# Local attention stack: ScalarE's copies ahead of the norm, the variance later in its step, three feed-forward tiles in the larger PSUM pool

## The chip, the core and the metric

The kernel runs on one core of one Trainium2 chip. The core has a matrix engine (TensorE, PE in the profile, its weight loads PEld), VectorE (DVE), ScalarE (ACT), GpSimd (POOL) and SyncE (SP, which here only issues transfers). Each engine takes its own instructions in the order of the program and waits for others on semaphores. [...]

The metric is the device time of one execution in microseconds. Before the change three runs gave 1410.27, 1412.57 and 1418.48; the median is 1412.57.

## The reference

`reference(x, ...)` is a decoder block over x of shape (2, 512, 128). It has three parts, each with a residual and a layer norm: a state-space layer with a mixture of experts, a cross attention, and a stack of local attention. The change touches only the third part, which takes more than half of the time. Cut to what matters:

```python
for i in range(6):                                   # DEPTH
    x = attn_layer(shift_tokens(x), Wqkv[i], ...) + x   # 16 heads of 64, windows of 32
    x = ffn_layer(shift_tokens(x), ln_g[i], ...) + x

def attn_layer(x, Wqkv, qs, ksc, Wo):
    q, k, v = split(x @ Wqkv)                        # 3 x 1024
    q, k = rotary(l2norm(q) * qs), rotary(l2norm(k) * ksc)
    # softmax(8 q k') v, each window of 32 looking at itself and the one before
    return local_attention(q, k, v) @ Wo

def ffn_layer(x, g, bln, W1, b1, W2, b2):
    mu = x.mean(-1); var = ((x - mu) ** 2).mean(-1)
    xn = (x - mu) / sqrt(var + 1e-5) * g + bln
    a, gate = split(xn @ W1 + b1)                    # 2 x 341
    return a * gelu(gate) @ W2 + b2
```

## The kernel before

All is float32. The activations lie transposed: 128 features on the partitions, tokens along the free axis. A tile is 128 tokens of one of two sequences, so a layer has eight tiles and six layers have 48. The stack is a software pipeline written out by hand, under a manual schedule: step s issues work for tile s (called A: projection, rotation, norms, values), for tile s-1 (B_: transposes of q and k, scores, softmax) and for tile s-2 (C: transposes of p, attention with v, transposes of o, output projection). The order of the calls in the step is the order on every engine.

After the last of the four tiles of a sequence a feed-forward begins. It takes two steps: F1, the step after, with `mean` and `var`, and F2, the next one, with `spread`, `hidden` and `out`. F2's `out` writes z, the input of the next layer's tiles. So the steps come in fours: F1, F2, and two without a feed-forward; I call such a group a block, and there are twelve, the last in the drain of the pipeline.

PSUM is split in two pools. `psa` has three buffers of two banks (128 x 1024 floats, tag "a"), which in a step go in turn to the q projection, the k projection, two attention outputs, the scores and the values. `psb` has two buffers of one bank (tag "b"), which go in turn to everything else: pairs of transposes, the FFN's mean, variance, spread, hidden pieces and outputs. A new tile waits until the readers of the tile that held its buffer before have finished.

What the change and the prediction touch, by line:

- `project` (L921, two projections of q and k on TensorE), `square` (L926, ScalarE), `rotate` (L933 and L937 on VectorE, the sum L942 on GpSimd), `sums` (L946, VectorE). rotate(0) is q's, rotate(1) k's.
- `norm`: ScalarE L964, L888, L889; GpSimd L965 and L890 to L893; then two products of 128x1024 on GpSimd (L968), whose results the next step's transposes of q and k (L1101) read.
- `values`: TensorE L954, ScalarE's copy L956, then two transfers issued by SP.
- `flip_p`, `flip_q`, `flip_k`: transposes L1101 and ScalarE's copies L1102. `flip_o`: transposes L1072, ScalarE's copies L1074 and L1076 to oT. `out` of a tile: L1091, every second tile, and VectorE L1094.
- `scores` L995 and L1006, `softmax` L1017 and L1019 on VectorE, `expo` L1023 on ScalarE, `attend` L1042, `weigh` L1056 and L1057 on VectorE.
- FFN: `mean` (`centre`: L1107, L1108, L1110), `var` (`rstd`: matmuls L1117, ScalarE L1119, L888, L889, GpSimd L890 to L893, giving ln_rs), `spread` (matmuls L1129 into ln_sd, VectorE L1147, GpSimd L1148), `table` (a table load on ScalarE, L1151), `hidden` (three chunks of 128, 128 and 85; each has a gate piece fg_ps L1158, a value piece fa_ps L1160, Gelu L1162 on ScalarE and the product L1163 on VectorE), `out` (L1172, L1175).

The end of the step as it was, with what the diff moves:

```python
A.norm()          # ScalarE, GpSimd
C.flip_o()        # TensorE, ScalarE
B_.expo()         # ScalarE
F1.var()          # TensorE, ScalarE, GpSimd
F2.out()
A.values()        # TensorE, ScalarE, SP
F1.table()
C.out()
```

Of the kernel before, what the change touches and what calls it, by code (L numbers as in the profile page):

```python
# [11 lines left out]
F32 = mybir.dt.float32  # L12
# [9 lines left out]
B, S, D = 2, 512, 128  # L22
NT = B * S
P = 128
# [8 lines left out]
INNER = H * DH  # L33
# [33 lines left out]
def decoder_kernel(ctx: ExitStack, tc: tile.TileContext, t: dict, out: bass.AP):  # L67
# [75 lines left out]
    def col(i, n=P):  # L143
        return cols[0:n, i : i + 1]
# [12 lines left out]
    def rstd(ss, name, scale=1.0 / D):  # L157

        v = fp.tile([P, NTB], F32, tag="v4", name=f"{name}_v", bufs=2)
        r = fp.tile([P, NTB], F32, tag="r4", name=f"{name}_r", bufs=2)  # L160
        na = fp.tile([P, NTB], F32, tag="n4", name=f"{name}_n", bufs=2)
        nc.gpsimd.tensor_scalar(v, ss, scale, EPS, ALU.mult, ALU.add)
        nc.gpsimd.tensor_tensor(r, v, mhalf.to_broadcast([P, NTB]), ALU.pow)
        nc.gpsimd.tensor_mul(na, v, r)
        nc.gpsimd.tensor_mul(na, na, r)
        nc.gpsimd.tensor_scalar(na, na, -0.5, 1.5, ALU.mult, ALU.add)
        nc.gpsimd.tensor_mul(r, r, na)
        return r
# [650 lines left out]
    def load_layer(i):  # L819
        wqkv = lw.tile([P, 3 * INNER], F32, tag="wqkv", name=f"wqkv_{i}")  # L820
        for j in range(3):
            sl = slice(j * INNER, (j + 1) * INNER)
            nc.sync.dma_start(out=wqkv[:, sl], in_=t["L0_ffn_Wqkv"][i][:, sl])
        wo = lw.tile([P, INNER // P, D], F32, tag="wo", name=f"wo_{i}")
        nc.sync.dma_start(out=wo, in_=t["L0_ffn_Wo"][i].rearrange("(c p) d -> p c d", p=P))
        w1 = lw.tile([P, 2 * DFF], F32, tag="w1", name=f"w1_{i}")
        nc.sync.dma_start(out=w1, in_=t["L0_ffn_W1"][i])
        w2 = lw.tile([P, 3, D], F32, tag="w2", name=f"w2_{i}")
        nc.sync.dma_start(
            out=w2[:, 0:2, :], in_=t["L0_ffn_W2"][i][0:256].rearrange("(c p) d -> p c d", p=P)  # L830
        )
        nc.sync.dma_start(out=w2[0 : DFF - 256, 2, :], in_=t["L0_ffn_W2"][i][256:DFF])

        qs = lw.tile([P, 4, DH], F32, tag="qs", name=f"qs_{i}", bufs=1)
        nc.sync.dma_start(out=qs, in_=t["qks"][i : i + 1].to_broadcast([P, 4, DH]))
        tab = lw.tile([P, 4, 4, DH], F32, tag="tab", name=f"tab_{i}")
        return wqkv, wo, w1, w2, tab, qs

    def scale_tables(layer):
        tab, qs = layer[4:]  # L840
        nc.gpsimd.tensor_mul(tab, rot, qs.unsqueeze(2).to_broadcast([P, 4, 4, DH]))
# [13 lines left out]
    psa = ctx.enter_context(tc.tile_pool(name="lpsa", bufs=3, space=PSUM))  # L855
    psb = ctx.enter_context(tc.tile_pool(name="lpsb", bufs=2, space=PSUM))
# [38 lines left out]
    def exp_ln_table():  # L895
        tc.keep_in_program_order(nc.scalar.preload_act_table_set("natural_log_exp_and_others"))
# [206 lines left out]

    def centre(dst, src):

        pm = psb.tile([P, S], F32, tag="b", name="ln_mean")
        mm(pm, ones_inv, src, start=True, stop=True)  # L1107
        nc.vector.tensor_sub(dst, src, pm)  # L1108
        sq = ftmp.tile([P, S], F32, tag="fsq", name="ln_sq")
        nc.scalar.activation(sq, dst, AF.Square)  # L1110
        return sq
# [12 lines left out]

    def spread(rs):

        sd = psb.tile([P, S], F32, tag="b", name="ln_sd")
        for n in range(NTB):
            mm(sd[:, n * P : (n + 1) * P], rs[:, n : n + 1].to_broadcast([P, P]), ident, start=True, stop=True)  # L1129
        return sd  # L1130

    class Ffn:
# [5 lines left out]
        def mean(self):  # L1138
            self.xc = ftmp.tile([P, S], F32, tag="xc", name="ln_xc")
            self.sq = centre(self.xc, za[:, self.b, 1 : 1 + S])  # L1140
# [4 lines left out]
        def spread(self):  # L1145
            xc, i = self.xc, self.i
            nc.vector.scalar_tensor_tensor(xc, xc, col(C_LNG + i), spread(self.rs), ALU.mult, ALU.mult)  # L1147
            nc.gpsimd.tensor_scalar_add(xc, xc, col(C_LNB + i))  # L1148
# [4 lines left out]
        def hidden(self):  # L1153
            i, xc, w1 = self.i, self.xc, self.w1
            hid = self.hid = ftmp.tile([P, 3, S], F32, tag="hid", name="fhid")
            for c, (f0, fs) in enumerate(FCH):
                pg = psb.tile([P, S], F32, tag="b", name="fg_ps")
                mm(pg[0:fs], w1[:, DFF + f0 : DFF + f0 + fs], xc, start=True, stop=True)  # L1158
                pa = psb.tile([P, S], F32, tag="b", name="fa_ps")
                mm(pa[0:fs], w1[:, f0 : f0 + fs], xc, start=True, stop=True)  # L1160
                ge = ftmp.tile([P, S], F32, tag="ge", name="ge", bufs=2)
                nc.scalar.activation(ge[0:fs], pg[0:fs], AF.Gelu, bias=col(C_B1 + 6 * i + 3 + c, fs))  # L1162
                nc.vector.scalar_tensor_tensor(  # L1163
                    hid[0:fs, c, :], pa[0:fs], col(C_B1 + 6 * i + c, fs), ge[0:fs], ALU.add, ALU.mult
                )
            exp_ln_table()
# [20 lines left out]
    with tc.manual_schedule(engines={ET.PE, ET.Activation, ET.DVE, ET.Pool}):  # L1187
        for s in range(len(tiles) + 5):
            A = B_ = C = None
            if s < len(tiles):  # L1190
                i, b, ti = tiles[s]
                if (b, ti) == (0, 0) and i + 1 < DEPTH:
                    layers[i + 1] = load_layer(i + 1)
                if (b, ti) == (1, 0) and i + 1 < DEPTH:
                    scale_tables(layers[i + 1])
                A = live[s] = Tile(s, i, b, ti, layers[i], live.get(s - 1))
            B_, C = live.get(s - 1), live.pop(s - 2, None)

            F1, F2 = ffns.get(s - 1), ffns.get(s - 2)
            if B_:  # L1200
                B_.keys_before()
            if A:
                A.begin()
                A.project(0)
                A.square(0)
            if F1:
                F1.mean()
            if F2:
                F2.spread()
            if A:  # L1210
                A.rotate(0)
            if C:
                C.flip_p()
            if A:
                A.project(1)
                A.square(1)
                A.rotate(1)
            if B_:
                B_.flip_q()
            if C:  # L1220
                C.attend()
                C.weigh()
            if B_:
                B_.flip_k()
            if A:
                A.sums(0)
                A.sums(1)
            if F2:
                F2.hidden()
            if B_:  # L1230
                B_.scores()
                B_.softmax()
            if A:
                A.norm()
            if C:
                C.flip_o()
            if B_:
                B_.expo()
            if F1:
                F1.var()  # L1240
            if F2:
                F2.out()
            if A:
                A.values()
            if F1:
                F1.table()
            if C:
                C.out()
                if C.ti == NTB - 1:
                    ffns[s] = Ffn(C.i, C.b, C.layer)  # L1250

    for b in range(B):
        y = ftmp.tile([P, S], F32, tag="xc", name="fin")
        for h0, at in ((0, 1), (64, 2)):
            nc.vector.tensor_add(
                y[h0 : h0 + 64], xT[h0 : h0 + 64, bs(b)], z[h0 : h0 + 64, b, at : at + S]
            )
        sd = spread(rstd(centre(y, y)))
        nc.vector.tensor_mul(y, y, sd)
        pt = psb.tile([P, 4, D], F32, tag="b", name="fin_t")  # L1260
        for n in range(4):
            tr(pt[:, n, :], y[:, n * P : (n + 1) * P], ident)
        yo = ftmp.tile([P, 4, D], F32, tag="ge", name="yo", bufs=2)
        nc.vector.tensor_copy(yo, pt)
        nc.sync.dma_start(out=out[b].rearrange("(n p) d -> p n d", p=P), in_=yo)
# [127 lines left out]
```

## Time and profile before

| | |
|---|---|
| median of three runs | 1412.57 us |
| profiled execution, its own time | 1412.37 us |
| its span, first to last instruction | 1410.6 us |
| mean granted TensorE clock | 0.910 |
| TensorE busy between 549 and 1330 us | 710.30 of 781.00 us |
| VectorE, ScalarE, GpSimd busy there | 496.18, 412.52, 430.80 us |
| first projection of tile 0, of tile 47 | 402.62 us, 1306.45 us |

The span is divided among engines by busy time. A busy share says how much of an engine's time is filled, not what ends last; that is read from the chain of waits (each piece is what the next one waited for) and from the timeline of one engine, where a bracket gives the idle time before an instruction and what ended it. Times in those views count from the start of the span, in us. "issue" is a wait that nothing in the profile explains. In the windows view each row is one stretch of time with the busy time of each engine, and after these the granted clock, from 0.50 to 1.00.

### The profile page before, as it was taken

The numbers are of one execution on the slowest core, as the hardware profiler recorded it, in microseconds if no ns is written. First come the engines' busy times: TensorE is split into PE (matmuls) and PEld (weight loads), VectorE is DVE, ScalarE is ACT, GpSimd is POOL, SyncE is SP. The second block draws the span as 40 slices with busy tenths as digits, with TensorE's granted clock in tenths as the row PEclk, the third lists the DMA queues.
The fourth block names the chain that finished last, engine by engine and source line by source line (L and its number), as shares of the span: only waits on it lengthen the run. The fifth ranks groups of instructions, "written<-read, shape, count | busy, mean of one in ns | idle before, by whom it ended". The sixth has DMA issues, their size and how long they took to land.

```text
span 1410.6 us, 37892 instructions
## 1 busy us (share of the span) xinstructions
PE 1171.2 (83%) x16553; PEld 744.0 (53%) x16553; DVE 856.9 (61%) x1125; ACT 635.5 (45%) x1110; POOL 733.7 (52%) x744
## 2 busy tenths in 40 slices
PE   6687688575468989898998989889998999998865
PEld 2223357565135646556565656556565655656543
DVE  2798685564347666566575666656665656667422
ACT  3533233132125555545555554545455555545521
POOL 2687562543467645556465555655455554546400
PEclk9888799697579999999999999999999989999976
DMA  4213665462401102111210102111211110101000
GB/s 115 69 62 95 174 178 162 148 205 75 156 16 33 39 26 73 48 32 32 73 48 26 53 18 73 47 32 35 71 47 32 29 32 29 31 15 33 28 1 16
DMA packets 51873, 88.52 MB, mean 63 GB/s; under 512 B 7070, under 2 KB 23836, under 8 KB 51708
## 3 DMA queue, kind: packets, MB, share of 16 engines
q1 hardware_dynamic: 46780, 76.78, 18.1%
q10 hardware_dynamic: 3456, 6.29, 1.8%
q0 software_dynamic: 1472, 3.02, 1.0%
q8 instruction: 131, 2.15, 0.6%
q14 instruction: 34, 0.28, 0.1%
HBM read 58.92 MB, written 3.19 MB: 44 GB/s over the span
## 4 chain that ended last, share of the span: by engine, by line
PE 53%; DVE 18%; ACT 7%; issue 5%; POOL 3%; DMA 2%; another core or an unknown queue 1%; SPq 0%; POOLq 0%; ACTq 0%; DVEq 0%
PE qk_ps L921 11%; PE wo_ps L1091 6%; PE v_ps L954 6%; PE t_ps L1101 5%; PE sim L1006 4%; DVE t L933 3%; DVE t L937 3%; DVE ss L946 3%; PE fa_ps L1160 3%; PE fg_ps L1158 2%; PE av L1042 2%; PE fo_ps L1172 2%; ACT sq L926 2%; PE gu_ps L530 2%; PE t_ps L1072 2%
## 5 line engine op out<-in xcount | busy, mean ns | idle before, releaser
L942 POOL TENSOR_TENSOR t<-t,t 128x1024 f32<-128x1024 f32 x96 | 227.3, 2371 | 203.7 <-DVE t L937 171.6
L921 PE MATMUL qk_ps<-wqkv,z 128*128 128x512 f32 x384 | 189.9, 619 | 1.8 <-POOL z L868 1.7
L968 POOL TENSOR_TENSOR t<-t,rn 128x1024 f32<-128x1024 f32 x96 | 180.6, 1903 | 3.8
L933 DVE TENSOR_TENSOR t<-qk_ps,tab 128x1024 f32<-128x1024 f32 x96 | 117.3, 1222 | 105.5 <-ACT sq L926 105.4
L926 ACT ACTIVATE sq<-qk_ps 128x1024 f32<-128x1024 f32 x96 | 98.5, 1027 | 117.6 <-PE qk_ps L921 112.8
L937 DVE TENSOR_TENSOR t<-qk_ps,tab 128x1024 f32<-128x1024 f32 x96 | 116.5, 1214 | 0.0
L921 PEld LDWEIGHTS qk_ps<-wqkv,z 128*128 128x128 f32 x384 | 74.3, 204 | 72.3 <-issue 68.8
L946 DVE TENSOR_REDUCE ss<-sq 128x16 f32<-128x1024 f32 x96 | 112.0, 1207 | 0.0
L1101 PE MATMUL t_ps<-ident,t 128*128 128x128 f32 x768 | 103.9, 279 | 6.5 <-POOL t L968 4.5
L1101 PEld LDWEIGHTS t_ps<-ident,t 128*128 128x128 f32 x768 | 87.0, 142 | 37.3 <-issue 24.2
L954 PE MATMUL v_ps<-wqkv,z 128*128 128x512 f32 x192 | 105.7, 679 | 0.0
L1006 PE MATMUL sim<-kT,qT 64*32 64x64 f32 x6144 | 78.5, 225 | 25.2 <-issue 25.0
L1006 PEld LDWEIGHTS sim<-kT,qT 64*32 64x32 f32 x6144 | 65.9, 105 | 50.3 <-issue 50.2
L1091 PE MATMUL wo_ps<-oT,wo 128*128 128x256 f32 x384 | 88.9, 385 | 1.5 <-ACT oT L1074 1.2
L306 PE MATMUL y<-hs,ident 128*128 128x512 f32 x128 | 77.8, 741 | 14.3 <-DVE hs L326 8.5
L1091 PEld LDWEIGHTS wo_ps<-oT,wo 128*128 128x128 f32 x384 | 72.9, 192 | 24.6 <-ACT oT L1074 8.9
L285 ACT ACTIVATE da<-dl,acol 128x512 f32<-128x512 f32 x64 | 43.9, 690 | 88.1 <-DVE hs L318 59.6
L965 POOL TENSOR_SCALAR ss<-ss 128x32 f32<-128x32 f32 x48 | 13.8, 288 | 130.6 <-ACT sc L964 130.5
L530 PE MATMUL gu_ps<-xT,w 128*128 128x128 f32 x480 | 71.6, 302 | 10.2 <-ACT xT L523 2.8
L1042 PE MATMUL av<-va,pT 64*32 64x65 f32 x3072 | 76.8, 228 | 3.2 <-issue 2.9
L1042 PE MATMUL av<-vb,pT 64*32 64x65 f32 x3072 | 76.6, 228 | 3.1 <-DVE t L937 2.3
L530 PEld LDWEIGHTS gu_ps<-xT,w 128*128 128x128 f32 x480 | 67.3, 215 | 18.6 <-issue 9.3
(263 smaller groups left out, 2303.3 us busy)
## 6 DMA issues: line engine op xcount, KB each, us to landing
w<-in_experts_dram SPq DMA_DIRECT2D x90, 256.0 KB
vb<-va SPq DMA_DIRECT2D x48, 390.0 KB
wqkv<-in_L_ffn_Wqkv_dram SPq DMA_DIRECT2D x18, 512.0 KB
vb<-va SPq DMA_DIRECT2D x36, 130.0 KB
b_sb<-bcd SPq DMA_DIRECT2D x16, 256.0 KB
b_sb<-bcd ACTq DMA_DIRECT2D x16, 256.0 KB
wo<-in_L_ffn_Wo_dram SPq DMA_DIRECT2D x6, 512.0 KB
c_sb<-bcd ACTq DMA_DIRECT2D x8, 256.0 KB
```

Source lines behind the costliest of these rows:

```text
L530: mm(pgu[:, (2 * m + i) * P : (2 * m + i + 1) * P], ws[k][:, w0 : w0 + P], xTs[k], start=True, stop=True,)
L921: mm(pa[:, hf * S : (hf + 1) * S], self.xb, w[:, w0 : w0 + S], start=True, stop=True)
L933: nc.vector.tensor_mul(t1, pa.rearrange("p (h d) -> p h d", d=DH), tab[:, 2 * qk, ti, :].unsqueeze(1).to_broadcast([P, H, DH]),)
L937: nc.vector.tensor_mul(t2.rearrange("p h (x d) -> p h x d", x=2), swap_halves(pa), tab[:, 2 * qk + 1, ti, :].rearrange("p (x d) -> p x d", ...
L942: nc.gpsimd.tensor_add(t1, t1, t2)
L946: nc.vector.tensor_reduce(self.ss[:, qk], self.sq[qk], AX.X, ALU.add)
L954: mm(pv[:, hf * S : (hf + 1) * S], self.xb, w[:, w0 : w0 + S], start=True, stop=True)
L968: nc.gpsimd.tensor_mul(self.rot[qk], self.rot[qk], self.rn[:, qk].unsqueeze(2).to_broadcast([P, H, DH]),)
L1006: mm(ps[32 * j : 32 * j + 32, par, hg, slot, :], qT[64 * r : 64 * r + 64, 2 * hg + c, WIN * w : WIN * (w + 1)], kT[64 * r : 64 * r + 64, 2 ...
L1042: mm(po[hh][32 * at : 32 * at + 32, g, i * DV : (i + 1) * DV], pT[rows, 4 * par + hg, 32 * j : 32 * j + 32], (self.v if par else self.v2)[ ...
L1091: mm(po, wo_l[:, c, :], self.oT[:, c, :], start=c == 0, stop=c == INNER // P - 1)
L1101: tr(pt[:, n, :], src[:, (4 * g + n) * P : (4 * g + n + 1) * P], ident)
```

## The change

The functions `centre` and `spread` take their PSUM tile from `psa` in place of `psb`; they use its first half. In `hidden`, chunk 1 takes one tile of `psa` for both its pieces, one in each half; chunks 0 and 2 keep two tiles of `psb`. In the step, `flip_o` is issued ahead of `norm`, which changes ScalarE's order (TensorE has nothing in `norm`), and `var` is issued after `values` and just ahead of `table`.

```diff
     def centre(dst, src):
 
-        pm = psb.tile([P, S], F32, tag="b", name="ln_mean")
+        pm = psa.tile([P, INNER], F32, tag="a", name="ln_mean")[:, 0:S]
...
     def spread(rs):
 
-        sd = psb.tile([P, S], F32, tag="b", name="ln_sd")
+        sd = psa.tile([P, INNER], F32, tag="a", name="ln_sd")[:, 0:S]
...
             for c, (f0, fs) in enumerate(FCH):
-                pg = psb.tile([P, S], F32, tag="b", name="fg_ps")
+                if c == 1:
+
+                    pga = psa.tile([P, 2, S], F32, tag="a", name="fga_ps")
+                    pg, pa = pga[:, 0], pga[:, 1]
+                else:
+                    pg, pa = (psb.tile([P, S], F32, tag="b", name=n) for n in ("fg_ps", "fa_ps"))
                 mm(pg[0:fs], w1[:, DFF + f0 : DFF + f0 + fs], xc, start=True, stop=True)
-                pa = psb.tile([P, S], F32, tag="b", name="fa_ps")
                 mm(pa[0:fs], w1[:, f0 : f0 + fs], xc, start=True, stop=True)
...
             if B_:
                 B_.scores()
                 B_.softmax()
+            if C:
+                C.flip_o()
             if A:
                 A.norm()
-            if C:
-                C.flip_o()
             if B_:
                 B_.expo()
-            if F1:
-                F1.var()
             if F2:
                 F2.out()
             if A:
                 A.values()
             if F1:
+                F1.var()
                 F1.table()
             if C:
                 C.out()
```

## The prediction

> **What bounds the kernel now.** I read the page first, then the chain of waits, then each engine's timeline over one block of four steps, then the same events in all the other blocks. The page says that TensorE leads and that the chain is half its work:
>
> ```profile
> PE 1171.2 (83%) x16553; PEld 744.0 (53%) x16553; DVE 856.9 (61%) x1125; ACT 635.5 (45%) x1110; POOL 733.7 (52%) x744
> ...
> PE 53%; DVE 18%; ACT 7%; issue 5%; POOL 3%; DMA 2%; another core or an unknown queue 1%; SPq 0%; POOLq 0%; ACTq 0%; DVEq 0%
> ```
>
> A share of 83% is an average with the front of the program. In the local stack the question is where TensorE stops. The steps come in fours: F1 (mean and variance of a feed-forward), F2 (its spread, hidden layer and output), then two without. Eleven such blocks run between 493 and 1336 us; the twelfth is the serial tail. In the block that starts at 886.78 us F1 and F2 take 46.71 us together. The chain of waits, in F1:
>
> ```profile
> 897.80 2.26 DVE ss L946 x2
> ...
> 900.09 0.33 ACT sc L964
> ...
> 901.02 0.48 ACT oT L1074
> ...
> 901.55 1.05 PE ln_var L1117 x8
> 902.60 2.55 PE v_ps L954 x4
> 905.15 2.69 PE qk_ps L921 x4
> ```
>
> VectorE's sums end at 900.06, ScalarE does the norm, only then copies oT, and the variance waits for that copy because it takes its PSUM buffer. TensorE's own timeline has the price (last bracket), and that of the transposes behind it:
>
> ```profile
> 898.10 1.09 PE L1072 MATMUL t_ps<-ident,o 128*128 128x128 f32 x8
> 901.55 1.05 PE L1117 MATMUL ln_var<-ones_inv,ln_sq 128*128 128x1 f32 x8 [2.35 <-ACT oT L1074]
> ...
> 909.57 0.66 PE L1101 MATMUL t_ps<-ident,s 128*128 128x128 f32 x4 [0.40 <-DVE ln_xc L1147]
> ...
> 919.37 1.12 PE L1160 MATMUL fa_ps<-ln_xc,w 128*128 128x512 f32 x2 [0.78 <-ACT ge L1162]
> ```
>
> **Copies ahead of the norm, variance late.** The transposes of o are issued from 898.10, the second copy can end 1.77 us after they start (924.30 to 926.07 in the F2 step), so at 899.9; the sums end at 900.06. The norm loses nothing here, and the 2.35 us wait goes. But what is late next? The spread, the second thing TensorE does in F2, needs ln_rs, which GpSimd makes after the norm's big products:
>
> ```profile
> 902.47 3.76 POOL L968 TENSOR_TENSOR t<-t,rn 128x1024 f32<-128x1024 f32 x2
> ...
> 907.04 0.20 POOL L893 TENSOR_TENSOR ln_rs<-ln_rs,ln_nv 128x4 f32<-128x4 f32 x1
> ```
>
> Nothing in the diff moves those. The norm follows the sums, the products follow the norm, ln_rs follows the products. Two blocks (493.1, 1289.0) show that limit bare: TensorE waits 1.15 us for ln_rs and starts ln_sd 20.52 us into F1. The typical block starts it at 20.90. So a removed 2.35 us buys 0.38. ScalarE's part of the variance, now behind the copy of v, ends about 17.8 us into F1 (softmax's exp at 902.9, 0.99 for the copy, three of 0.23), and the products end at 19.46 - 0.34, so moving it costs nothing while that 1.3 us lasts. No DMA is moved late: the copy of v, which SP's two transfers wait for, ends near 903.8 instead of 906.2.
>
> **The mean's buffer.** The transposes of p wait 0.34 us in every F1 because the mean holds one of two buffers; in the larger pool it takes one of three, whose last reader (softmax, 884.1) is long done. Everything up to the sums moves 0.34 us earlier, and ln_sd with it: 20.52 - 0.34 = 20.18. The added allocations shift the rotation: attention's first output now waits for rotate(0) (892.5) and is reached at 893.1; nothing new is late.
>
> **Where the moved norm hurts.** It now waits for the copies, that is for TensorE. If the transposes start later than 12.94 - 1.79 = 11.15 us into F1 (12.94 is 13.28, the end of the sums, less 0.34), ln_sd is later by as much. In the blocks at 965.9, 1047.1, 1129.2 and 1209.9 they start at 13.24, 13.48, 14.06 and 13.58, after stalls of about 2 us marked "issue". Summing min by block (before: 20.52, 20.90, 20.90, 22.47, 20.90, 20.90, 20.90, 22.14, 24.04, 22.50, 20.52; after: 20.18 plus that delay) gives gains of 0.1, 0.7, 0.7, 2.1, 0.4, 0.7, -1.0, 0.0, 1.3, 0.2 and 0.3: **5.6 us** over eleven blocks. In the two steps without a feed-forward the same delay is covered: the products have 1 us or more before the next step's transposes want them.
>
> **F2.** From ln_sd to the step's end is 25.8 us in nearly every block. The spread in the larger pool removes the 0.40 wait. The hidden layer takes 6.78 us from its first matmul to the scores (six pieces of 0.86 plus waits). With the middle chunk in the larger pool, five pieces run without a stop (4.3 us) and the sixth waits for chunk 0's product on VectorE, which follows the sums: 6.28 + 0.80 = 7.08 us after rotate(1) starts, end at 7.98, against 9.32 (35.59 - 26.27) now. That is 1.34. The middle chunk's buffer waits for rotate(1) (2.35 us after its start; reached at 4.3), so no new stall. What follows keeps its order, the copies of oT still stand before the output's matmul. 0.40 + 1.34 = 1.74, times 11 = **19.1 us**. Output waits in the fourth step (0.32, 0.49, 0.40 in three blocks) give **1.2**; the tail's hidden layer, about **1.1**, an estimate from its waits at 1376 and 1378 us. Sum before the clock: **27.0 us**.
>
> **The clock.** TensorE in F1 no longer stops at the variance but runs on to the end of F2's first projection, some 16.3 us into F1 (transposes of o from 11.0, then 0.87 + 1.72 + 0.9 + 1.72), and waits there until 20.2: one hole of 3.9 us in place of 2.35. The trace says what holes do; its drops of the granted clock last 3.41 us or multiples. Columns: stretch, length, busy time of PE, PEld, DVE, ACT, POOL, clock, DMA:
>
> ```profile
> 586.12:589.54 3.42, 1.27 (x9) 1.19 (x10) 3.01 (x3) 2.17 (x6) 1.60 (x6) 1.00 0.00 0
> 589.54:592.95 3.41, 3.41 (x5) 1.33 (x4) 0.00 (x0) 1.58 (x5) 3.41 (x3) 0.50 0.00 0
> ...
> 504.20:507.61 3.41, 1.74 (x78) 1.41 (x54) 3.38 (x4) 1.09 (x4) 1.17 (x3) 1.00 0.02 5
> ```
>
> All seven stretches of that grid between 493 and 1313 us with under 1.6 us of TensorE work were followed by a stretch at half clock (586.12 is one); of those with 1.7 to 2.4, some. Half clock costs half the stretch: at 902.60 the two projections took 2.55 + 2.69 instead of 2 x 1.72, 1.8 us more. Today that falls where ln_rs is late anyway. After the change it falls on ln_sd, the transposes of p and the second projection, all on the path. [...] By the trace a stretch left with under 1.6 us of work is enough, and a 3.9 us hole always makes one. Averaged over where the grid falls: 6% of the time two half stretches (2.4 us lost), 54% one that begins inside the hole (1.24), 40% a whole one (1.7): 1.5 us a block, **16.5 us**. If 2.4 us of work were enough too, it is 2.0 a block, 22.5. I take the trace: measured here, and nearest. [...]
>
> **Sum.** 27.0 - 16.5 = 10.5. Profiled execution: span 1410.6, its own time 1412.37; the median shown is 1412.57, so the same level. 1412.4 - 10.5 = **1402 us**.
>
> **Rivals.**
> A, the above: 1402 (1394 to 1408 with the penalty at 0.8 to 2.0 us a block). Chance 0.50.
> B, the clock hardly pays: either holes become shorter or drops fall in the wait itself. For it: 1.74 us of work at 504.20 without a drop, and today's drops cost little of the block (46.7 us with or without one). Time 1385; if the supply stalls in F1 also vanish, 1378. Chance 0.25.
> C, the throttle takes everything: two half stretches after each hole, 11 x 2.4 = 26.4, time 1412. For it: double drops (6.83 us) exist in this trace. Against: of the eleven drops between 549 and 1330 us seven last one stretch. Chance 0.12.
> D, slower: the norm behind the copies. Place: ScalarE in F1; price: one for one beyond 11.15 us; if supply stalls put o's transposes at 14.06 in every F1, as in the worst block, the delay is 2.57 x 11 = 28.3 instead of 9.1 us, time 1421. It decides against the change once the mean delay passes 0.83 + 0.95 = 1.8 us a block. Against: only four of eleven blocks do it now, and the order of TensorE's stream barely changes. Chance 0.13.
>
> **How the numbers follow.** About 0.5% (7 us) is what can be told from no change, so faster means under 1405.5. A is two thirds faster, one third within; B faster; C within; D slower: 0.58, 0.29, 0.13. The range leaves about 0.1 each side: 1380 to 1419, A's own 1394 to 1408.
>
> **What would show it.** Right: no wait of ln_var for oT; a new wait of about 4 us of ln_sd for ln_rs (a line that hardly exists today); half clock following it in F2; no 0.34 and 0.40 waits at the transposes; the scores some 8.0 us after rotate(1). Wrong: ln_sd earlier than 20 us into F1, or full clock after the hole (B); scores no earlier in F2; norm ends late by ScalarE waiting for t_ps (D).

## The result, and the profile after

The changed kernel takes 1403.6 us (median of 20 runs, 1397.57 to 1411.25); the kernel before, run beside it, takes 1413.44 us (20 runs). The ratio is 0.9936, with a 95% interval from 0.9915 to 0.9957: the change makes it faster by 0.6%, or 9 us. The forecast was 1402 us.

The page, which sums up the profiled execution (span 1399.6 us, before 1410.6), shows little of it. Busy times are nearly what they were, but in the chain VectorE has lost three points and GpSimd has gained five:

```profile
PE 1153.5 (82%) x16553; PEld 750.1 (54%) x16553; DVE 858.4 (61%) x1125; ACT 632.2 (45%) x1110; POOL 732.8 (52%) x744
...
PE 53%; DVE 15%; POOL 8%; ACT 7%; issue 6%; DMA 1%; POOLq 0%; ACTq 0%; DVEq 0%
```

4.1 us of the 11.0 between the two spans lie ahead of the local stack (its first projection starts at 398.5 in place of 402.6), where the change is not; so the stack itself shows 6.9.

Why GpSimd has come in is seen in TensorE's timeline of the block that starts at 571.24:

```profile
584.88 0.95 PE L1117 MATMUL ln_var<-ones_inv,ln_sq 128*128 128x1 f32 x8
585.69 1.96 PE L921 MATMUL qk_ps<-wqkv,z 128*128 128x512 f32 x4
591.19 2.08 PE L1129 MATMUL ln_sd<-ident,ln_rs 128*128 128x128 f32 x8 [3.53 <-POOL ln_rs L893]
593.05 1.79 PE L1101 MATMUL t_ps<-ident,s 128*128 128x128 f32 x8
```

The variance waits for nothing, and neither do the transposes of p (the waits of 2.35, 0.34 and 0.40 us are gone). In their place stands one wait of 3.53 us, for ln_rs. And what follows it is slow: the spread takes 2.08 us and the transposes 1.79. In the kernel before, block at 886.78, the spread took 1.05 us and the transposes 0.60 and 0.66, the second four after their wait:

```profile
907.67 1.05 PE L1129 MATMUL ln_sd<-ident,ln_rs 128*128 128x128 f32 x8
908.57 0.60 PE L1101 MATMUL t_ps<-ident,s 128*128 128x128 f32 x4
```

The windows view of the changed kernel's stretch, on the grid of the clock (columns: stretch, length, busy time of PE, PEld, DVE, ACT, POOL, then the clock, and last the DMA engines' busy share and GB/s):

```profile
587.75:591.16 3.41, 0.00 (x0) 0.00 (x0) 0.00 (x0) 3.32 (x6) 3.16 (x7) 1.00 0.48 131
591.17:594.58 3.41, 3.39 (x16) 3.40 (x17) 1.28 (x2) 0.56 (x2) 0.72 (x2) 0.50 0.10 33
...
816.45:819.86 3.41, 1.71 (x4) 0.40 (x3) 0.15 (x1) 3.14 (x6) 3.33 (x3) 1.00 0.05 16
819.86:823.27 3.41, 1.67 (x15) 1.67 (x16) 0.47 (x1) 1.73 (x3) 1.77 (x6) 1.00 0.54 150
```

Here a stretch with 0.00 us of TensorE work is followed by one at a clock of 0.50, and that one holds the spread. In the block at 801.5 the grid cuts a hole of 3.44 us in two (the last two rows): the stretches keep 1.71 and 1.67 us of work, and the clock stays at 1.00, in the stretch behind them (823.27) too.

### The profile page after: what moved, and what is told of

Same layout as the page of the kernel before. It is cut to its first block, busy times and chain, and to the rows that moved or that the text cites. A ratio compares the mean times of both kernels' runs of the same rounds, so it can differ in the third digit from the quotient of the medians.

```text
span 1399.6 us, 37893 instructions
## 1 busy us (share of the span) xinstructions
PE 1153.5 (82%) x16553; PEld 750.1 (54%) x16553; DVE 858.4 (61%) x1125; ACT 632.2 (45%) x1110; POOL 732.8 (52%) x744
## 3 DMA queue, kind: packets, MB, share of 16 engines
q8 instruction: 131, 2.15, 0.7%
## 4 chain that ended last, share of the span: by engine, by line
PE 53%; DVE 15%; POOL 8%; ACT 7%; issue 6%; DMA 1%; POOLq 0%; ACTq 0%; DVEq 0%
PE qk_ps L921 8%; PE wo_ps L1091 6%; PE t_ps L1101 6%; PE sim L1006 5%; PE v_ps L954 4%; POOL t L968 3%; PE t_ps L1072 3%; DVE t L933 3%; PE av L1042 3%; DVE t L937 3%; PE fo_ps L1176 2%; ACT sq L926 2%; PE gu_ps L530 2%; PE fg_ps L1163 2%; PE sim L995 2%
## 5 line engine op out<-in xcount | busy, mean ns | idle before, releaser
L921 PE MATMUL qk_ps<-wqkv,z 128*128 128x512 f32 x384 | 186.6, 610 | 1.9 <-POOL z L868 1.7
L968 POOL TENSOR_TENSOR t<-t,rn 128x1024 f32<-128x1024 f32 x96 | 180.5, 1901 | 3.8
L933 DVE TENSOR_TENSOR t<-qk_ps,tab 128x1024 f32<-128x1024 f32 x96 | 117.3, 1221 | 97.6 <-ACT sq L926 97.6
L921 PEld LDWEIGHTS qk_ps<-wqkv,z 128*128 128x128 f32 x384 | 70.7, 197 | 59.9 <-issue 56.1
L954 PE MATMUL v_ps<-wqkv,z 128*128 128x512 f32 x192 | 98.5, 638 | 1.2 <-issue 1.2
L306 PE MATMUL y<-hs,ident 128*128 128x512 f32 x128 | 76.4, 732 | 15.8 <-DVE hs L326 9.3
L1074 ACT COPY oT<-t_ps 128x512 f32<-128x512 f32 x48 | 28.1, 585 | 134.4 <-PE t_ps L1072 134.4
L1091 PEld LDWEIGHTS wo_ps<-oT,wo 128*128 128x128 f32 x384 | 72.9, 190 | 20.2 <-issue 9.0
L1102 ACT COPY kT<-t_ps 128x512 f32<-128x512 f32 x96 | 51.7, 589 | 64.0 <-PE t_ps L1101 64.0
```

Of the source, the lines that this page charges most:

```text
L921: mm(pa[:, hf * S : (hf + 1) * S], self.xb, w[:, w0 : w0 + S], start=True, stop=True)
L933: nc.vector.tensor_mul(t1, pa.rearrange("p (h d) -> p h d", d=DH), tab[:, 2 * qk, ti, :].unsqueeze(1).to_broadcast([P, H, DH]),)
L954: mm(pv[:, hf * S : (hf + 1) * S], self.xb, w[:, w0 : w0 + S], start=True, stop=True)
L968: nc.gpsimd.tensor_mul(self.rot[qk], self.rot[qk], self.rn[:, qk].unsqueeze(2).to_broadcast([P, H, DH]),)
L1091: mm(po, wo_l[:, c, :], self.oT[:, c, :], start=c == 0, stop=c == INNER // P - 1)
```

## The experiments

Each ratio is to the kernel before, run beside it on the same chip. To set them side by side, the last column takes 1413.4 us as the time before, so 0.01 is 14.1 us.

| | ratio, 95% interval | against before |
|---|---|---|
| the changed kernel | 0.9936 [0.9915, 0.9957] | -9.0 us |
| e1_fill: with useless matmuls in the hole | 0.9837 [0.9808, 0.9866] | -23.0 |
| e2_early: variance early | 0.9635 [0.9604, 0.9667] | -51.6 |
| e3_noswap: copies behind the norm again | 0.9808 [0.9774, 0.9842] | -27.1 |
| e4_nohid: middle chunk in the smaller pool | 1.0048 [1.0024, 1.0073] | +6.8 |
| e5_early_noswap: e2 and e3 | 0.9572 [0.9530, 0.9613] | -60.5 |
| e6_swap_alone on the kernel before | 1.0026 [1.0008, 1.0044] | +3.7 |
| e7_psum_alone on the kernel before | 0.9819 [0.9779, 0.9859] | -25.6 |
| e8_late_alone on the kernel before | 0.9964 [0.9944, 0.9984] | -5.1 |
| e9_swap_f1: copies ahead in F1 only | 0.9918 [0.9887, 0.9950] | -11.6 |
| e10_swap_notf1: copies ahead except in F1 | 0.9795 [0.9766, 0.9823] | -29.0 |
| e11_fill_noswap: e1 and e3 | 0.9798 [0.9766, 0.9829] | -28.6 |

**e1_fill: does the hole's clock cost time?** Work that nobody reads, where TensorE would stand idle:

```diff
             xc, i = self.xc, self.i
+            idle = psb.tile([P, S], F32, tag="b", name="idle")
+            for _ in range(3):
+                mm(idle, ones_inv, za[:, self.b, 1 : 1 + S], start=True, stop=True)
             nc.vector.scalar_tensor_tensor(xc, xc, col(C_LNG + i), spread(self.rs), ALU.mult, ALU.mult)
```

> The changed kernel with three useless matmuls (the mean's operands, 512 columns, 0.86 us each, 2.6 us in all) between F2's first projection and the spread, where TensorE sits idle for ln_rs. Theory (the 3.5 us hole drops the clock, and that costs 1.2 to 1.5 us a block): the granted clock in F2 is 1.00 in nearly every block, ln_sd does not start later in the blocks with a whole hole, and although 31 us of work are added the time falls to about 1390 us (1385 to 1396). Rival (the drop falls where it costs nothing): no gain, 1403 to 1409.

It is 14 us faster than the changed kernel, about 1390 us as expected. TensorE's timeline, block at 655.2 (each of the three useless matmuls makes two records):

```profile
671.56 2.74 PE L1149 MATMUL idle<-za,ones_inv 128*128 128x512 f32 x6
675.18 1.16 PE L1129 MATMUL ln_sd<-ident,ln_rs 128*128 128x128 f32 x8 [0.88 <-POOL ln_rs L893]
676.17 1.04 PE L1101 MATMUL t_ps<-ident,s 128*128 128x128 f32 x8
```

ln_sd still starts 19.96 us into F1, because ln_rs is ready no sooner, but the spread and the transposes take 1.16 and 1.04 us in place of 2.08 and 1.79. The granted clock is 1.00 in all eleven F2 steps, and from ln_sd to the end of F2 it is 23.9 to 24.0 us in every one of the first ten, where the changed kernel has 25.3 on average. So the clock behind the hole does cost time.

**e2_early: is it the norm's products that ln_rs stands behind?** The variance goes to where its input is long ready:

```diff
             if C:
                 C.attend()
                 C.weigh()
+            if F1:
+                F1.var()
             if B_:
                 B_.flip_k()
...
             if F1:
-                F1.var()
                 F1.table()
```

> The changed kernel with the FFN's variance issued after attention in F1, ahead of the transposes of k, so that GpSimd makes ln_rs before the norm's two big products. Theory (ln_sd waits for ln_rs because that stands behind L968): ln_sd starts some 16.5 us into F1 in place of 20, the hole and the clock drop are gone, F1 and F2 take about 40.5 us in place of 45.5, and the time is about 1352 us (1345 to 1365). Rival (F2 is then held by the next thing, the products L968 that the transposes of q want, or VectorE): a gain of at most 15 us, 1388 to 1400.

The ratio of 0.9635 is 1362 us on the scale of the expectation, inside its range. GpSimd's timeline and TensorE's, block at 643.1:

```profile
655.24 0.20 POOL L893 TENSOR_TENSOR ln_rs<-ln_rs,ln_nv 128x4 f32<-128x4 f32 x1
...
658.68 3.76 POOL L968 TENSOR_TENSOR t<-t,rn 128x1024 f32<-128x1024 f32 x2
```

```profile
657.29 1.88 PE L921 MATMUL qk_ps<-wqkv,z 128*128 128x512 f32 x4
659.00 1.05 PE L1129 MATMUL ln_sd<-ident,ln_rs 128*128 128x128 f32 x8
659.89 1.04 PE L1101 MATMUL t_ps<-ident,s 128*128 128x128 f32 x8
```

ln_rs is made ahead of the products, and ln_sd follows the projection at once, 15.9 us into F1. F1 and F2 take 41.1 to 42.0 us in the first five blocks (40.5 expected), and 43.1 to 46.3 in the five from 859.9 to 1171.8, which have stalls marked "issue" in F1.

**e3_noswap, e9 and e10: what is the swap worth?**

```diff
-            if C:
-                C.flip_o()
             if A:
                 A.norm()
+            if C:
+                C.flip_o()
```

> The changed kernel with flip_o behind norm again, the other edits kept. Theory (with the variance behind the values the copies are no longer waited for, and the norm behind them costs ln_rs in the blocks where TensorE is late): ln_sd starts near 20.0 us in every block, 17.9 us less over eleven blocks of the profile of after, some of it given back to the clock; about 1392 us (1386 to 1399). Rival (the copies ahead of the norm are what brings the gain): 1408 to 1415.

Without the swap the changed kernel is 18 us faster, 1386 us on the scale, at the edge of what was expected. In F1 of the block at 1035.4 (changed) ScalarE's timeline reads

```profile
1050.43 0.59 ACT L1074 COPY oT<-t_ps 128x512 f32<-128x512 f32 x1 [4.59 <-PE t_ps L1072]
1051.29 0.58 ACT L1076 COPY oT<-t_ps 128x512 f32<-128x512 f32 x1 [0.27 <-PE t_ps L1072]
1051.77 0.33 ACT L964 ACTIVATE sc<-ss,tiny 128x32 f32<-128x32 f32 x1
```

and in e3, block at 1037.2:

```profile
1049.94 0.32 ACT L964 ACTIVATE sc<-ss,tiny 128x32 f32<-128x32 f32 x1 [2.31 <-DVE ss L946]
...
1052.19 0.59 ACT L1074 COPY oT<-t_ps 128x512 f32<-128x512 f32 x1 [1.31 <-PE t_ps L1072]
```

The norm starts 16.3 us into F1 with the swap and 12.8 without, although the sums are done at 12.71 in both: ScalarE stood 4.59 us in front of TensorE's transposes with the norm queued behind. The mean start of ln_sd is 21.60 us with the swap and 20.62 without, so 10.8 us over eleven blocks and not the 17.9 expected: without the swap the last five blocks are still late (20.2 to 23.3 us). Two kernels place the cost in a step; the diff is e9's, and e10 has the two conditions exchanged:

```diff
-            if C:
+            if C and F1:
                 C.flip_o()
             if A:
                 A.norm()
+            if C and not F1:
+                C.flip_o()
```

> The changed kernel, flip_o ahead of norm in the F1 steps alone. Theory (the cost of the swap is made in F1, through ln_rs and the hole behind it): like the changed kernel, a ratio of 0.992 to 0.995. Rival (it is made in the other steps, where the norm's products feed the next transposes of q and k): like e3, 0.979 to 0.983.

> The changed kernel, flip_o ahead of norm in all steps but F1. Theory: like e3, a ratio of 0.979 to 0.983. Rival: like the changed kernel, 0.992 to 0.995.

They gave 0.9918 (0.992 to 0.995 was expected) and 0.9795: the cost is made in F1, and in the other steps the swap costs nothing that can be told.

**e11_fill_noswap: late norm or clock?** e1's three matmuls and e3's order together; the edits are those above.

> e1's useless matmuls in the kernel of e3 (flip_o behind norm). With the hole filled the clock cannot drop behind it, so the difference from e1 is what the late norm costs by itself. Theory (some 10 of the 18 us between the changed kernel and e3 are late norms, the rest is clock): 5 to 10 us under e1, a ratio of 0.977 to 0.980. Rival (all of it is clock): equal to e1, 0.984.

The ratio is 0.9798, 5.5 us under e1, but the two intervals overlap. With the clock out of the question (1.00 in all eleven F2 steps) ln_sd starts at 20.57 us on average against e1's 21.40, 9 us over eleven blocks of these two profiles. So part of the 18 us is probably the late norm and the rest the clock; the split is known only roughly. Against e3 the useless work brings nothing measurable: that profile has holes of 2.88 us in its early blocks and one drop in eleven F2 steps. That is not a safe length of hole: e10 has the same holes (2.86 us) and the clock dropped in four of its F2 steps. Three of the early blocks of e3 last about 75 us, nearly 22 stretches of the clock's grid, so there the cut falls at nearly the same place block after block.

**e4_nohid: what is the middle chunk worth?** In the changed kernel TensorE writes both its pieces to one PSUM tile, fga_ps, which ScalarE (L1166) and VectorE (L1167) read, each once a block; e4 takes that tile away:

```diff
-                if c == 1:
-
-                    pga = psa.tile([P, 2, S], F32, tag="a", name="fga_ps")
-                    pg, pa = pga[:, 0], pga[:, 1]
-                else:
-                    pg, pa = (psb.tile([P, S], F32, tag="b", name=n) for n in ("fg_ps", "fa_ps"))
+                pg, pa = (psb.tile([P, S], F32, tag="b", name=n) for n in ("fg_ps", "fa_ps"))
```

> The changed kernel with the hidden layer's middle chunk in the smaller PSUM pool again. Theory (that chunk is worth 1.34 us a block): from rotate(1) to the scores 9.3 us in place of 8.0, time 1403.6 + 15 = about 1418 us (1414 to 1422). Rival (the hidden layer is held by VectorE in any case): 1403 to 1407.

The ratio is 1.0048 against 0.9936: 15.8 us, slower even than the kernel before. From rotate(1) (VectorE, L933) to the scores (L995, whose masks are bf16) it is 9.3 us again, as before; the changed kernel has 8.0. First the changed kernel, block at 801.5, where the middle chunk waits for nothing, then e4, block at 813.2:

```profile
826.45 1.22 DVE L933 TENSOR_TENSOR t<-qk_ps,tab 128x1024 f32<-128x1024 f32 x1 [0.64 <-ACT sq L926]
...
831.65 1.02 PE L1164 MATMUL fga_ps<-ln_xc,w 128*128 128x512 f32 x2
...
834.47 0.60 PE L995 MATMUL sim<-masks,hot 32*128 32x512 bf16 x2
```

```profile
839.78 1.23 DVE L933 TENSOR_TENSOR t<-qk_ps,tab 128x1024 f32<-128x1024 f32 x1 [1.97 <-ACT sq L926]
...
846.10 1.12 PE L1159 MATMUL fa_ps<-ln_xc,w 128*128 128x512 f32 x2 [0.78 <-ACT ge L1161]
...
849.09 0.60 PE L995 MATMUL sim<-masks,hot 32*128 32x512 bf16 x2
```

The chunk itself makes 1.3 us a block, some 14 us over eleven. But in e4's profile all of the first ten F2 steps are below full clock (0.945 to 0.948), in the changed kernel's seven of them (0.89 to 0.95), so the clock can have a part in the 15.8 us.

**e5_early_noswap: with an early variance, does the swap still cost?** Both edits of e2 and e3.

> The early variance of e2 with flip_o behind norm, as in e3. Theory (the copies' place costs only through ln_rs, and with the early variance ln_rs no longer stands behind the norm): the same as e2, about 1358 us on the scale where before is 1413 (1352 to 1364). Rival (the norm behind the copies also holds the transposes of q and k in the next step): 8 us or more below e2.

The ratio is 0.9572, the fastest of all; it beats both kernels. On the scale it is 1353 us, inside the theory's range, but it lies 9 us under e2, as the rival has it; the two intervals overlap a little, so neither is settled. The rival's mechanism does not show: in e2 no transposes of q or k in F2 wait for L968. What differs between the two profiles is F1 in the later blocks, where e2 has more half clock (0.75 to 0.91 in six blocks; e5 has three below 1.00), and the stalls of TensorE marked "issue", 38.1 us in e2 and 26.8 in e5 between 480 and 1330 us. Whether the swap makes these is open.

**e6, e7, e8: each part alone on the kernel before.** e6 has the swap, e7 the three PSUM edits, e8 the variance behind the values, each as in the diff of the change.

> The kernel before with one edit: flip_o ahead of norm. Theory (it takes the 2.35 us wait of ln_var away and lays it before ln_sd, delays ln_rs where TensorE is late, and the larger hole drops the clock in F2): slower than before by 5 to 25 us, ln_sd at 20.5 us into F1 or later. Rival (a removed wait of 2.35 us in eleven blocks is a gain): 20 us or more faster.

> The kernel before with the three PSUM edits alone (mean, spread and middle chunk in the larger pool), the order of the step as it was. Theory: 1.34 + 0.40 in F2 and 0.35 to 0.55 in F1 for each of eleven blocks, 23 to 25 us faster, 1389 us on the scale of 1413 (1384 to 1396). Rival (the PSUM edits need the new order to pay): 1405 or more.

> The kernel before with the variance behind the values alone. Theory (the values cover 1.7 of the 2.35 us wait, but ln_sd waits for ln_rs at 20.5 us into F1 instead of starting at 20.5 to 24.0): ln_sd at 20.5 in nearly every block, 5 to 12 us faster. Rival (moving the variance late makes ln_rs late): slower by 5 us or more.

The swap alone is slower by 3.7 us, a little less than expected, with ln_sd at a mean of 21.60 us (before 21.52) and five F2 steps at a mean clock of 0.95: it moves most of the 2.35 us wait to ln_sd, and nothing is gained. The PSUM edits alone bring 25.6 us, where 23 to 25 were expected; so the two edits of the order together take 16.6 of them away again. In the first six blocks of e7 ln_sd starts at 20.35 us, only 0.40 later than the 19.95 of the changed kernel, and the half clock falls on F1's work ahead of ln_rs, where it costs little: from ln_sd to the end of F2 it is 23.9 to 24.1 us. The late variance brings 5.1 us. PSUM and variance about add up: -25.6 - 5.1 = -30.7 against the -27.1 of e3. The swap on top of those two takes 18 us away, far more than the 3.7 alone. In the profiles it puts the mean start of ln_sd off by 0.98 us there and by 0.08 on the kernel before, where TensorE itself reaches ln_sd late in three of the four blocks with stalls (22.1 to 24.0 us); why it costs more there was not tested further.

## Why the prediction was right

- **The wait moves to ln_rs.** Forecast: from 2.35 us at ln_var to about 3.9 at ln_sd, starting near 20.18 us. The profile has 3.44 to 3.54 us in the five clean blocks, with a start at 19.95 to 20.20. e2 shows the cause that was named, the products on GpSimd.
- **The mean's buffer.** A gain of 0.34 us was forecast; the second projection and the sums come 0.56 us earlier.
- **The F1 sum of 5.6 us was mis-sized.** It measured -0.9: the mean start of ln_sd is 21.60 after and 21.52 before. The mechanism, a norm late where TensorE is late, was on the table and priced one for one, but the delays of before were carried over. After the change the last five blocks are late, not four: those at 1197.0 and 1277.5 have two stalls each in F1 (1.71 and 2.27, 1.49 and 2.31) and start ln_sd at 24.2 and 24.7. Against 19.95 the mean delay is 1.65 us, not 0.83. The price that rival D set (the norm behind the copies) was thus half paid, and e3, e9 and e10 show that it is real.
- **The stalls marked "issue".** No run varied them, but the two traces point to their source: the page lists 131 packets of queue q8, 2.15 MB of the kind "instruction", and each of the 12 (before) and 18 (after) stalls of TensorE over 1 us between 480 and 1330 us ends 1.19 to 1.63 us after such a packet has come in; of stalls at random times about one in eighteen would, as 108 packets come in that time. So TensorE seems to wait for its own program there, as the prediction's word "supply stalls" supposes. All its "issue" stalls in that time add up to 28.1 us before and 38.3 after.
- **F2.** A gain of 1.74 us a block was forecast. Without a drop of the clock, ln_sd to the end of F2 takes 24.0 us in place of 25.8, so 1.8. The middle chunk's 1.34 shows as 8.0 against 9.3 us from rotate(1) to the scores, and e4 fits it (15.8 us over the program).
- **The clock.** A loss of 16.5 us was forecast from the trace before, where all seven stretches with under 1.6 us of TensorE work were followed by half clock. Seven of eleven F2 steps are clearly below full clock after (0.89 to 0.95), and filling the hole returns 14 us (the profile has 12.5: 277.3 us from ln_sd to the ends of F2, less eleven times 24.0 and one stall of 0.8). The profile after shows nearly the same bound: between 480 and 1335 us all ten stretches of the changed kernel's grid that were left with 0.00 to 1.53 us of TensorE work were followed by half clock, and only two of them were wholly idle (587.75 and 741.35). Of the eight with 1.58 to 1.96 us three were, so the prediction's bound of 1.6 us is close but not exact.
- **Rivals.** B, the clock that hardly pays, fell with e1. C, two half stretches after each hole, did not occur: of the thirteen drops between 480 and 1335 us eleven last one stretch and two last two. D did occur in part.

The errors have opposite signs: F1 gave 6.5 us less than forecast and the clock took 2.5 less (4.0 by the profile), so part of the good agreement of 1402 and 1403.6 is luck. In the profiles, F1 and F2 of the first ten blocks take 474.8 us before and 466.2 after; the eleventh loses 4.2 us at ln_sd and wins 1.9 behind it: 6.3 us together, of the 10.5 - 2.3 = 8.2 forecast for them (2.3 is the fourth step's and the tail's share). Sorted by edit, the forecast's own terms gave the PSUM edits 19.1 + 0.34 x 11 + 2.3 = 25.1 us and left the two order edits with a loss of 14.6; e7 and the changed kernel have 25.6 and 16.6. The prediction held the change's better part in its numbers, and did not say so.

## What to carry to other kernels

When an edit removes a wait, look for the next thing that the same engine waits for and what that stands behind; here four small GpSimd instructions behind 3.76 us of products held TensorE, and moving their source a few lines up was worth nearly five times what the whole change brought (42.6 us against 9.0). Price the parts of a change one by one: here one part alone (25.6 us) beat the whole. On ScalarE, which ran its instructions in the order of the calls, an instruction put ahead of an unrelated one lends it its own waits: the copies were ready early in a good block, but in a late one they held the norm (16.3 in place of 12.8 us into F1). Price a hole on TensorE by what runs just behind it too, and test that by filling it with work that nobody reads (14 us in e1).

## What the runs showed of the hardware

31 us of added useless matmuls made the program 14 us faster (e1): in the changed kernel the clock granted behind the hole fell to 0.50 in seven of eleven blocks, for 3.41 us in six of them and for twice that in one; with the holes filled it was 1.00 in all eleven F2 steps. Where the hole fell on the clock's grid made the difference between two blocks: 3.44 us cut into stretches with 1.71 and 1.67 us of work left the clock at 1.00 at 816.45 (F2's second projection starts 1.87 us after ln_sd), and a stretch with 0.00 us at 587.75 cost 1.6 us (F2's second projection starts 23.44 us into F1 there, 21.87 in the block at 490.9 without a drop, with ln_sd at 19.95 and 20.00).
